# Attention inverses spread by transfer, a reordered hand-over to the MLP, a later record of sums and earlier sums for the last MLP group

## The chip, the cores and the metric

One core of a Trainium2 chip runs the whole program. The metric is the time of one execution on the device in microseconds; the median of three runs is 951.97 us (951.22 to 953.68). The engines are named as the profile names them: PE is TensorE (its matrix products; PEld its weight loads), DVE is VectorE, ACT is ScalarE, POOL is GpSimd, SP is SyncE, which here only issues transfers. A letter q behind an engine's name means its instruction queue.

## The reference

A batch of B = 16 sequences of S = 256 tokens with D = 256 features passes three attention layers and one MLP. All have H = 16 heads of 16 features; all numbers are 32-bit.

```python
# layer 0: cross attention to y, with RMS norms
x = rmsnorm(x + softmax(rms(x) Wq (rms(y) Wk)^T / 4) (rms(y) Wv) Wo)
# layer 1: causal self attention, layer norm, biases, rotary positions
x = x + attn(ln1(x), ln1(x), causal) @ sa_wo + sa_bo
# layer 2: cross attention to y, layer norm, biases, rotary positions
x = x + attn(ln2(x), y) @ ca_wo + ca_bo
# MLP: 256 -> 1024 -> 256
x = x + gelu(ln3(x) @ fc1_w + fc1_b) @ fc2_w + fc2_b
```

The layers follow one another for each sequence, but the sequences are independent.

## The kernel before, in words

There are 48 attentions, three for each sequence. `ORDER` fixes by hand in which order their layers come, so that attention i+1, i+2 and so on always belong to other sequences and can be prepared while attention i runs. No scheduler reorders anything: each engine executes its instructions in the order in which the loops issue them, and waits at each one until its operands are there.

**One attention** (`class Att`). Queries and keys are kept with features on the partitions: `qm` holds each query twice with every second head set to zero, `kT` the keys. `scores(n)` does one block: 8 products into two PSUM tiles `S` (two such pairs of banks exist, so a new block needs the exponentials of the block before last), ACT writes the exponentials to `pt`, and for the causal layer POOL zeroes what lies above the diagonal (L494). `values(n)` multiplies `pt` with `va`, the values of a head with a column of ones behind them, into the single PSUM bank `A`, so that the row 16 of each head's 32 rows is the sum of the exponentials. ACT copies `A` to `av` (L529). A cross attention has 4 such blocks, a causal one 3.

**Division by the sums.** The sums lie in 8 of the 128 rows of `av`. They are sent to memory (`hop[0]`, L530) and read back as a dense tile `sums` of 128 x 32 (L539); eight more transfers (L544) collect the unnormalized outputs into `oT`, features on partitions. `invert` takes the reciprocals on DVE (L554), adds `sums` to the record `seen` on POOL (L555), writes the reciprocals to `hop[1]` (L556) and reads them into one row out of 16 of the tile `first` (L560). `divide` repeats each such row over the 16 rows of its head by a stream shuffle on DVE (L566) and multiplies `oT` (L570). `project` multiplies with the output weights (L307) and adds to `x` (L576, L579). `seen` is examined once, in the MLP: if a sum was not finite, a second, safe version of the attentions runs instead.

**The loop over attentions.** Step i runs the blocks of attention i and between them, on all engines, pieces of its neighbours: after block 0 the finishing of i-3, statistics and normalization of i+2, `divide` of i-2 and the queries of i+1; after block 1 the keys of i+1; after the last but one the values of i+1 and `invert` of i-1; after the last `project` of i-2 and the transposes (`turn`) of i+2. Queries and keys go through a chain on DVE after their product (L406 to L435: shuffle, two multiplications with the rotary tables, an addition, for queries two more), and the next step's first scores need both. The last values of an attention run in the step after it.

**The MLP** works on groups of two sequences (`class Mlp`, 8 groups), both products split by Strassen's scheme with seven products instead of eight: `up(1)` to `up(7)` and `down(1)` to `down(7)`. Each has a normalization (`stats`, `norm`), transposes into `hT` (`turn`), and a `mix` of four subtractions on DVE (L672). The `up` products share PSUM banks: `X` and `Z` are summed into by several products and read between them; ACT copies a partial result out (`keep_sum`, L695), DVE adds to one (`add_sum`, L700), ACT applies GELU (L707). `sum_a(1)` to `sum_a(4)` are the DVE sums of GELU results (L757) that the `down` products need. `down` also sums into a bank `X` (the bank `A`) and a bank `Z`, which DVE reads after each product (`begin`, L779; `end`, L783). The products `up` of the next group run ahead of the `down` products of this one; the last group has none to run ahead. The end of the attentions and the first MLP groups are joined by hand: `mlps[0].stats()` and `norm()` in step 46, its `turn` and `mix` in step 47, `mlps[1].stats()` and `norm()` at its end, then the `up` products of group 0 with `project` of attention 46 between them, `turn` of group 1, its `up` products with `project` of attention 47 between them.

## Time and profile before

| | |
|---|---|
| runs, median (lowest to highest) | 951.97 us (951.22 to 953.68) |
| profiled execution | 953.16 us, of it 951.4 us span |
| PE busy | 936.1 us, 98% of the span |
| DVE, ACT, POOL busy | 666.0, 571.9, 294.6 us |
| shuffle of the inverses, DVE L566 | 48 x 0.742 us |
| record of sums, POOL L555 | 48 x 0.320 us; 280.4 us idle just before them |
| share of time in which the 16 DMA engines are busy, 40 to 720 us | 0.18 |
| from the last attention's first scores to the first `down` product | 721.10 to 767.14 us |

The profile is one execution. Its span runs from the first to the last instruction. A busy PE is not PE at its peak: its products are pipelined and their ends are modelled, so the distance between the starts of neighbouring groups says more than the busy share. Idle time of an engine that does not hold the others up costs nothing.

### The profile page before, as it was taken

The numbers are of one execution on the slowest core, as the hardware profiler recorded it, in microseconds if no ns is written. First come the engines' busy times: TensorE is split into PE (matmuls) and PEld (weight loads), VectorE is DVE, ScalarE is ACT, GpSimd is POOL, SyncE is SP. The second block draws the span as 40 slices with busy tenths as digits, with TensorE's granted clock in tenths as the row PEclk, the third lists the DMA queues.
The fourth block names the chain that finished last, engine by engine and source line by source line (L and its number), as shares of the span: only waits on it lengthen the run. The fifth ranks groups of instructions, "written<-read, shape, count | busy, mean of one in ns | idle before, by whom it ended". The sixth has DMA issues, their size and how long they took to land.

```text
span 951.4 us, 30022 instructions
## 1 busy us (share of the span) xinstructions
PE 936.1 (98%) x12374; PEld 551.6 (58%) x12374; DVE 666.0 (70%) x1483; ACT 571.9 (60%) x821; POOL 294.6 (31%) x502
## 2 busy tenths in 40 slices
PE   8999999999999999999999999999999899999997
PEld 4444455445454545455454445445445699999997
DVE  4347768877776797677866768787776776667653
ACT  4666666766666766666766676666676634444440
POOL 4213454334334344144242423334112211222200
PEclk9999999999999999999999999999999999999999
DMA  9531221202121122110222101010101000000001
GB/s 316 171 97 29 78 71 32 71 18 79 25 70 28 42 54 73 24 33 19 72 71 74 32 22 27 19 29 21 26 21 26 13 24 23 13 12 23 23 24 47
DMA packets 66089, 46.96 MB, mean 49 GB/s; under 512 B 25364, under 2 KB 65044, under 8 KB 65944
## 3 DMA queue, kind: packets, MB, share of 16 engines
q1 hardware_dynamic: 64712, 43.89, 16.8%
q8 instruction: 100, 1.64, 0.7%
q10 hardware_dynamic: 1232, 1.07, 0.4%
q14 instruction: 45, 0.37, 0.1%
HBM read 26.54 MB, written 5.79 MB: 34 GB/s over the span
## 4 chain that ended last, share of the span: by engine, by line
PE 88%; DVE 5%; DMA 3%; POOL 1%; ACT 1%; issue 1%; SPq 0%; DVEq 0%; POOLq 0%
PE S L476 18%; PE A L515 17%; PE d L294 16%; PE d L307 15%; PE A L762 6%; PE upX L676 6%; PE downZ L762 3%; PE upZ L676 3%; PE d L274 2%; PE d L762 2%; PE d L676 1%; DMA hop<-av 1%; DVE a L410 1%; PE d L657 1%; DVE u L410 1%
## 5 line engine op out<-in xcount | busy, mean ns | idle before, releaser
L487 ACT ACTIVATE pt<-S 128x1024 f32<-128x1024 f32 x224 | 217.4, 1022 | 114.3 <-PE S L476 114.3
L476 PE MATMUL S<-qm,kT 32*128 32x512 f32 (+1 forms) x1536 | 202.9, 600 | 2.1 <-DVE kT L435 1.0
L515 PE MATMUL A<-pt,va 128*32 128x256 f32 (+1 forms) x3072 | 193.0, 367 | 1.3 <-POOL pt L494 0.8
L515 PEld LDWEIGHTS A<-pt,va 128*32 128x32 f32 x3072 | 80.5, 109 | 158.5 <-issue 95.4
L487 ACT ACTIVATE pt<-S,sy 128x1024 f32<-128x1024 f32 x128 | 135.7, 1111 | 46.1 <-PE S L476 44.0
L555 POOL TENSOR_TENSOR seen<-seen,sums 128x64 f32<-128x64 f32 x48 | 15.4, 320 | 280.4 <-DVE sums L554 185.8
L476 PEld LDWEIGHTS S<-qm,kT 32*128 32x128 f32 x1536 | 62.4, 183 | 68.5 <-issue 25.4
L494 POOL TENSOR_SCALAR_AFFINE_SELECT pt<-pt 128x512 f32<-128x512 f32 x128 | 88.5, 713 | 27.4 <-ACT pt L487 27.3
L283 POOL TENSOR_TENSOR cur<-cur,bias 128x512 f32<-128x512 f32 x48 | 65.3, 1365 | 58.9 <-DVE xn L263 58.9
L402 ACT ACTIVATE a<-d,qk_bias 128x256 f32<-128x256 f32 x128 | 53.8, 471 | 38.5 <-PE d L294 33.4
L294 PE MATMUL d<-hT,sa 128*32 128x256 f32 x1024 | 63.1, 379 | 0.0
L238 POOL TENSOR_SCALAR r_ln<-bmv 128x2 f32<-128x2 f32 x48 | 12.6, 261 | 153.3 <-DVE bmv L257 152.6
L529 ACT COPY av<-A 128x512 f32<-128x512 f32 x96 | 56.6, 590 | 3.5 <-PE A L515 3.2
L410 DVE TENSOR_TENSOR u<-u,turn 128x512 f32<-128x512 f32 x64 | 53.5, 836 | 0.0
L410 DVE TENSOR_TENSOR a<-a,turn 128x512 f32<-128x512 f32 x64 | 50.2, 784 | 2.2
L263 DVE TENSOR_SCALAR xn<-cur,bmv,r_ln 128x256 f32<-128x256 f32 x96 | 51.1, 579 | 0.8 <-POOL r_ln L239 0.6
L707 ACT ACTIVATE g<-g,fb 128x256 f32<-128x256 f32 x96 | 40.9, 497 | 15.4 <-DVE g L700 15.4
L579 DVE TENSOR_TENSOR cur<-d,cur 128x512 f32<-128x512 f32 x32 | 21.7, 679 | 38.8 <-PE d L307 38.7
L406 DVE STREAM_SHUFFLE u<-a 128x512 f32<-128x512 f32 x64 | 47.7, 746 | 0.0
L294 PEld LDWEIGHTS d<-hT,sa 128*32 128x32 f32 x1024 | 34.3, 110 | 22.1
L695 ACT COPY g<-upX 128x512 f32<-128x512 f32 x32 | 17.2, 589 | 46.8 <-issue 39.0
L757 DVE TENSOR_TENSOR g<-g,g 128x512 f32<-128x512 f32 x64 | 40.7, 681 | 0.0
(142 smaller groups left out, 1568.1 us busy)
## 6 DMA issues: line engine op xcount, KB each, us to landing
oT<-av SPq DMA_DIRECT2D x384, 32.0 KB
cur<-in_x SPq DMA_DIRECT2D x16, 256.0 KB
xT<-in_xt SPq DMA_DIRECT2D x16, 256.0 KB
yT<-in_yt SPq DMA_DIRECT2D x16, 256.0 KB
y<-in_y SPq DMA_DIRECT2D x16, 256.0 KB
out<-res SPq DMA_DIRECT2D x15, 256.0 KB
fc<-in_fc SPq DMA_DIRECT2D x2, 1024.0 KB
rq<-rq_hop SPq DMA_DIRECT2D x14, 128.0 KB
```

Of the source, the lines that this page charges most:

```text
L283: nc.gpsimd.tensor_tensor(t, t, bias_sb[:, row : row + D].unsqueeze(1).to_broadcast([P, NC, D]), ALU.add)
L294: nc.tensor.matmul(ps[j : j + 32, t * S : (t + 1) * S], lhsT=w[:, k, at + t * P + j : at + t * P + j + 32], rhs=src[:, k, :], start=(k == ...
L307: nc.tensor.matmul(ps[j : j + 32, c * D : (c + 1) * D], lhsT=src[:, k, c * P + j : c * P + j + 32], rhs=w[:, k, at : at + D], start=(k == ...
L402: nc.scalar.activation(a[:, t], ps[:, t], AF.Identity, bias=bias[:, t : t + 1])
L410: nc.vector.tensor_tensor(t, t, table.unsqueeze(1).to_broadcast([P, KC, S]), ALU.mult)
L476: nc.tensor.matmul(ps[:, j, 2 * m * u : 2 * m * (u + 1)] .rearrange("p (i s) -> p i s", i=2), lhsT=self.kT[r, t, kc * P : (kc + 1) * P], r ...
L487: nc.scalar.activation(pt[:, :, :w], ps[:, :, :w], AF.Exp, scale=scale)
L494: nc.gpsimd.affine_select(out=diag, in_=diag, compare_op=ALU.is_ge, fill=0.0, base=0, pattern=[[0, 2], [0, 2], [1, P]], channel_multiplier=-1,
L515: nc.tensor.matmul(self.av[32 * r : 32 * r + 32, i, q0:S], lhsT=self.va[:, kc, 8 * t + 2 * r + i, :], rhs=pts[r // 2][:, r % 2, i * m : (i ...
L529: nc.scalar.copy(av, self.av)
L676: nc.tensor.matmul(banks[c // 2][:, (c % 2) * S : (c % 2 + 1) * S], lhsT=a[:, c * P : (c + 1) * P], rhs=b, start=(first and c % 2 == 0), s ...
L762: nc.tensor.matmul(ps[:, c, :], lhsT=a[f // 2][:, f % 2, c * P : (c + 1) * P], rhs=b[:, f, :], start=(first and c == 0 and f == 0), stop=True,
```

## The change

Four things are changed.

- **Inverses.** The tile `first` and the shuffle are gone. `invert` now reads `hop[1]` back with two transfers, one for each 128 features, which repeat each head's row of 256 inverses over 16 partitions: two times 128 x 256 numbers in place of 16 rows of 256. `divide` multiplies `oT` with this tile.
- **Record of sums.** The addition to `seen` moves from `invert` to `divide`, about one step later.
- **The end of the attentions.** The statistics, normalization and transposes of MLP groups 0 and 1 come one or two places earlier (steps 45, 46 and 47), their transposes are copied out of PSUM by DVE instead of ACT, `up(2)` of group 0 runs inside the last attention, `project` of attention 45 moves from the last block of step 47 to its second, and the `up` products, GELUs, `mix` and divisions behind the loop are put in a new order. `up(1)` and `up(2)` can now come in either order (`keep_or_add`). GELUs are named as steps of their own (`ups`).
- **The last group.** Its `sum_a(1)` to `sum_a(3)` are issued between the `down` products of the group before, in tiles of other tags.

The warm-up products at the start read a tile of zeros that is allocated later, as `first` is gone.

```diff
-    firsts = []
-    for i in range(2):
-        first = ctile([P, KC, S], f"first_{i}")
-        nc.gpsimd.memset(first, 0.0)
-        firsts.append(first)
     dram = ctx.enter_context(tc.tile_pool(name="dram", bufs=2, space=bass.MemoryType.DRAM))
     vas = [ctile([P, NC, H, 32], f"va_{i}") for i in range(2)]
...
+    zeros = work.tile([P, 512], F32, tag="inv", name="zeros")
+    nc.gpsimd.memset(zeros, 0.0)
     idle = dense_ps()
     for n in range(2):
         nc.tensor.matmul(
-            idle, lhsT=ident, rhs=firsts[0].rearrange("p t s -> p (t s)"), start=True, stop=True
+            idle, lhsT=ident, rhs=zeros, start=True, stop=True
         )
...
             if self.layer == 0:
                 nc.vector.tensor_scalar(sums[:, 0], sums[:, 0], 1e-30, None, ALU.max)
             nc.vector.reciprocal(sums[:, 1], sums[:, 0])
-            nc.gpsimd.tensor_tensor(seen, seen, sums, ALU.add)
             nc.sync.dma_start(
                 out=self.hop[1].rearrange("t g (a b) -> (t g a) b", b=2 * H), in_=sums[:, 1]
             )
-            self.first = firsts[self.i % 2]
-            nc.sync.dma_start(
-                out=self.first[0:P:HD], in_=self.hop[1].rearrange("t g q -> g t q")
-            )
+            self.inv = work.tile([P, KC, S], F32, tag="inv", name="inv")
+            for t in range(KC):
+                nc.sync.dma_start(
+                    out=self.inv[:, t],
+                    in_=self.hop[1, t].unsqueeze(1).to_broadcast([8, HD, S]),
+                )
         def divide(self):
-            inv = work.tile([P, KC, S], F32, tag="inv", name="inv", bufs=1)
-            nc.vector.stream_shuffle(
-                inv.rearrange("p t s -> p (t s)"),
-                self.first.rearrange("p t s -> p (t s)"), FIRST,
-            )
-            nc.vector.tensor_tensor(self.oT, self.oT, inv, ALU.mult)
+            nc.gpsimd.tensor_tensor(seen, seen, self.sums, ALU.add)
+            nc.vector.tensor_tensor(self.oT, self.oT, self.inv, ALU.mult)
         def project(self):
             res = by_token(self.oT, self.w_o, 0)
...
+            self.a = {}
             self.xs = [rows_of(2 * g + i) for i in range(2)]
         def stats(self):
...
-        def turn(self):
+        def turn(self, copy=nc.scalar.copy):
             self.hT = self.pool.tile([P, KC, 2, S], F32, tag="qm", name="hT3")
             for i, xn in enumerate(self.xns):
                 ps = dense_ps()
...
-                nc.scalar.copy(self.hT[:, :, i, :], ps.rearrange("p (k s) -> p k s", s=S))
-        def mix(self):
+                copy(self.hT[:, :, i, :], ps.rearrange("p (k s) -> p k s", s=S))
+        def mix(self, tag="av"):
             b = self.hT
-            self.ts = self.pool.tile([P, 4, S], F32, tag="av", name="ts")
-            t1, t2, t3, t4 = (self.ts[:, i] for i in range(4))
+            if tag == "av":
+                ts = self.pool.tile([P, 4, S], F32, tag=tag, name="ts")
+                self.ts = [ts[:, i] for i in range(4)]
+            else:
+                pairs = [self.pool.tile([P, 2, S], F32, tag=tag, name="ts") for _ in range(2)]
+                self.ts = [t[:, i] for t in pairs for i in range(2)]
+            t1, t2, t3, t4 = self.ts
             for o, x, y in (
                 (t1, b[:, 0, 1], b[:, 0, 0]), (t2, b[:, 1, 1], t1),
                 (t3, b[:, 1, 1], b[:, 0, 1]), (t4, b[:, 1, 0], t2),
...
-        def half(self, i, j):
+        def half(self, i, j, tag=None):
+            if tag is not None:
+                t = self.pool.tile([P, 4, S], F32, tag=tag, name=f"g{i}{j}")
+                return [t[:, 0:2], t[:, 2:4]]
             if i == 0:
                 return [
                     self.pool.tile([P, 2, S], F32, tag="yT", name=f"g{i}{j}", bufs=Y_LIVE)
...
-        def gelu(self, i, j, banks=None):
+        def keep_or_add(self, i, j, banks):
+            (self.add_sum if (i, j) in self.a else self.keep_sum)(i, j, banks)
+        def gelu(self, i, j):
+            banks = self.X if (i, j) == (0, 1) else None
             for c in range(4):
                 t = self.a[i, j][c // 2][:, c % 2]
                 src = t if banks is None else banks[c // 2][:, (c % 2) * S : (c % 2 + 1) * S]
...
         def up(self, n):
-            b, ts = self.hT, self.ts
+            b, ts = self.hT, getattr(self, "ts", None)
             if n == 1:
-                self.a = {}
                 self.X = psS.tile([P, 2, 512], F32, tag="S", name="upX")
                 self.X = [self.X[:, i] for i in range(2)]
                 self.up_product(1, self.X, up_a(0, 0), b[:, 0, 0], True)
-                self.keep_sum(0, 0, self.X)
+                self.keep_or_add(0, 0, self.X)
             elif n == 5:
                 self.Z = psS.tile([P, 2, 512], F32, tag="S", name="upZ")
                 self.Z = [self.Z[:, i] for i in range(2)]
-                self.up_product(5, self.Z, up_s[0], ts[:, 0], True)
+                self.up_product(5, self.Z, up_s[0], ts[0], True)
                 self.keep_sum(1, 1, self.Z)
             elif n == 6:
-                self.up_product(6, self.X, up_s[1], ts[:, 1], False)
+                self.up_product(6, self.X, up_s[1], ts[1], False)
                 self.keep_sum(1, 0, self.X)
             elif n == 2:
                 w = [dense_ps() for _ in range(2)]
                 self.up_product(2, w, up_a(0, 1), b[:, 1, 0], True)
-                self.add_sum(0, 0, w)
-                self.gelu(0, 0)
+                self.keep_or_add(0, 0, w)
             elif n == 7:
-                self.up_product(7, self.X, up_a(1, 0), ts[:, 2], False)
+                self.up_product(7, self.X, up_a(1, 0), ts[2], False)
                 self.add_sum(1, 1, self.X)
-                self.gelu(1, 1)
             elif n == 3:
                 self.up_product(3, self.Z, up_s[2], b[:, 1, 1], False)
                 self.add_sum(1, 0, self.Z)
-                self.gelu(1, 0)
             elif n == 4:
-                self.up_product(4, self.X, up_a(1, 1), ts[:, 3], False)
+                self.up_product(4, self.X, up_a(1, 1), ts[3], False)
                 self.a[0, 1] = self.half(0, 1)
-                self.gelu(0, 1, self.X)
-        def sum_a(self, n):
+        def ups(self, *steps):
+            for n in steps:
+                if isinstance(n, tuple):
+                    self.gelu(*n)
+                else:
+                    self.up(n)
+        def sum_a(self, n, tags=(None, None)):
             if n == 1:
-                self.s = {1: self.half(1, 2), 2: self.half(1, 3), 3: self.a[1, 0]}
+                self.s = {1: self.half(1, 2, tags[0]), 2: self.half(1, 3, tags[1])}
+                self.s[3] = self.a[1, 0]
                 self.s[4] = self.s[2]
             x, y, op = {
                 1: (self.a[1, 0], self.a[1, 1], ALU.add),
...
                     do(i - 2, "divide")
                     if not finishing:
                         do(i + 2, "norm")
+                    if i == N_ATT - 3:
+                        mlps[0].stats()
+                    if i == N_ATT - 2:
+                        mlps[0].norm()
+                    if i == N_ATT - 1:
+                        mlps[0].turn(nc.vector.tensor_copy)
                     do(i + 1, "q")
                 elif n == 1:
                     do(i + 1, "k")
...
                         do(i + 2, "norm")
                     for j in kept.get(i, ()):
                         att(j).keep()
+                    if i == N_ATT - 1:
+                        do(i - 2, "project")
+                        mlps[1].norm()
                 if n == final - 1:
                     do(i + 1, "v")
                     do(i - 1, "invert")
                     do(i + 2, "send")
+                    if i == N_ATT - 2:
+                        mlps[1].stats()
+                    if i == N_ATT - 1:
+                        mlps[0].up(2)
+                        mlps[0].mix("hT")
                 if n == final:
-                    do(i - 2, "project")
+                    if i == N_ATT - 1:
+                        mlps[1].turn(nc.vector.tensor_copy)
+                    else:
+                        do(i - 2, "project")
                     do(i + 2, "turn", "receive")
                 if i == 0 and n == 0:
                     load(4)
...
                     fold_gain(fc1_sb, slice(0, FF), V_G3, [i // 8])
                 if n == 1 and i > 8 and not a.causal:
                     next(combined, None)
-                if i == N_ATT - 2 and n == 1:
-                    mlps[0].stats()
-                    mlps[0].norm()
-                if i == N_ATT - 1 and n == 2:
-                    mlps[0].turn()
-                    mlps[0].mix()
-                if i == N_ATT - 1 and n == 3:
-                    mlps[1].stats()
-                    mlps[1].norm()
         last = att(N_ATT - 1)
         last.values(-1)
+        mlps[0].up(1)
         do(N_ATT - 2, "divide")
-        for n in (1, 5, 6, 2):
-            mlps[0].up(n)
+        mlps[0].ups(5, 6, (0, 0))
         do(N_ATT - 2, "project")
+        mlps[1].mix()
         last.invert()
-        for n in (7, 3, 4):
-            mlps[0].up(n)
-        mlps[1].turn()
-        mlps[1].mix()
+        mlps[0].ups(7, (1, 1), 3, 4, (0, 1), (1, 0))
         for g in range(B // 2):
             this = mlps[g]
             ahead, next_but_one = (mlps[i] if i < B // 2 else None for i in (g + 1, g + 2))
-            if ahead is not None:
+            if g == 0:
+                ahead.ups(2, 1)
+            elif ahead is not None:
                 ahead.up(1)
-            this.sum_a(1)
             if g == 0:
                 last.divide()
+            if ahead is not None:
+                this.sum_a(1)
             if next_but_one is not None:
                 next_but_one.stats()
             if ahead is not None:
-                ahead.up(5)
-                ahead.up(6)
-            this.sum_a(2)
+                ahead.ups(5, 6)
+                this.sum_a(2)
+            if g == 0:
+                ahead.gelu(0, 0)
+                last.project()
+            elif ahead is not None:
+                ahead.ups(2, (0, 0))
             if ahead is not None:
-                ahead.up(2)
-            if g == 0:
-                last.project()
-            if ahead is not None:
-                ahead.up(7)
-                ahead.up(3)
-                ahead.up(4)
-            this.sum_a(3)
+                ahead.ups(7, (1, 1), 3, (1, 0), 4, (0, 1))
+                this.sum_a(3)
             this.down(1)
+            final = g == B // 2 - 2
             if next_but_one is not None:
                 next_but_one.norm()
+            if final:
+                ahead.sum_a(1, ("qm", "av"))
             this.down(5)
+            if final:
+                ahead.sum_a(2)
             this.down(6)
             this.sum_a(4)
             this.down(2)
             if next_but_one is not None:
                 next_but_one.turn()
                 next_but_one.mix()
+            if final:
+                ahead.sum_a(3)
             this.down(7)
             this.down(3)
             this.down(4)
```

More of the change, by code (lines that the diff above doesn't have):

```diff
@@ L42 @@
 NROW = 6 * D
-FIRST = [i // HD * HD for i in range(32)]
 SWAP = [(i // HD) * HD + (i + HD // 2) % HD for i in range(32)]
@@ L1029, in xattn_kernel @@
                 m.mix()
-                for n in (1, 5, 6, 2, 7, 3, 4):
-                    m.up(n)
+                m.ups(1, 5, 6, 2, (0, 0), 7, (1, 1), 3, (1, 0), 4, (0, 1))
                 for n in (1, 2, 3):
```

## The prediction

> **What bounds the kernel now.** I read the page's first two parts, then the instructions in order of time at the places where TensorE's rows stand apart, then who waited for whom. The first two parts:
>
> ```profile
> span 951.4 us, 30022 instructions
> PE 936.1 (98%) x12374; PEld 551.6 (58%) x12374; DVE 666.0 (70%) x1483; ACT 571.9 (60%) x821; POOL 294.6 (31%) x502
> PEclk9999999999999999999999999999999999999999
> ```
>
> TensorE is busy almost throughout and its granted clock never drops; no other engine is above 70%. Since the changed kernel has the same products, each as long as before, only time in which TensorE does not advance can be won. To see it, I compare the distance between the starts of neighbouring groups with the same distance where nothing waits: a score group (S) 1.07 us, a value group (A) 0.89, a projection 1.84, an `up` product 1.73, eight transposes 0.87. Almost all groups keep these distances. The time lost sits in three places. First, from the last attention to the first `down` product:
>
> ```profile
> 721.10 1.14 PE L476 MATMUL S<-qm,kT 32*128 32x512 f32 x8
> 723.41 2.04 PE L476 MATMUL S<-qm,kT 32*128 32x512 f32 x8 [0.17 <-ACT pt L487]
> ...
> 739.68 1.89 PE L676 MATMUL d<-hT,fc 128*128 128x256 f32 x8
> 742.86 1.93 PE L307 MATMUL d<-cao,oT 128*32 128x256 f32 x32 [1.29 <-issue]
> 750.01 1.04 PE L657 MATMUL d<-ident,xn 128*128 128x128 f32 x8
> 752.88 1.99 PE L676 MATMUL upX<-hT,fc 128*128 128x256 f32 x8 [1.84 <-ACT hT L661]
> 767.14 1.95 PE L762 MATMUL A<-fc,g 128*128 128x128 f32 x16
> ```
>
> Columns: start, duration, engine, line, operation, count, and in brackets the idle time and its releaser. The second score group took 2.04 us where 1.14 is usual, because it waited for the exponentials; 739.68 to 742.86 is 3.19 us for a 1.73 us step; 750.01 to 752.88 is 2.87 for 0.87. Second, the value groups that follow a causal mask:
>
> ```profile
> 343.23 0.32 POOL L555 TENSOR_TENSOR seen<-seen,sums 128x64 f32<-128x64 f32 x1 [3.77 <-DVE sums L554]
> 343.50 1.41 POOL L494 TENSOR_SCALAR_AFFINE_SELECT pt<-pt 128x512 f32<-128x512 f32 x2
> 344.97 0.36 PEld L515 LDWEIGHTS A<-pt,va 128*32 128x32 f32 x10 [0.56 <-POOL pt L494]
> ```
>
> GpSimd stands 3.77 us at `seen`, waiting for VectorE's reciprocals; the two masks behind it come late, and the value group's weight load waits for them. Third, the boundary into the last MLP group:
>
> ```profile
> 933.30 3.69 DVE L757 TENSOR_TENSOR g<-g,g 128x512 f32<-128x512 f32 x6
> 933.53 2.02 PE L762 MATMUL A<-fc,g 128*128 128x128 f32 x16 [0.61 <-DVE res L779]
> 937.38 2.05 PE L762 MATMUL A<-down_t,g 128*128 128x128 f32 x16
> ```
>
> Last, the rows that the new transfer must be priced from:
>
> ```profile
> 300.62 0.64 SPq L560 DMA_DIRECT2D first<-hop  x1
> 302.65 0.01 DVE L566 LOAD_MASK_SELECT inv<-first  x1 [0.85 <-DMA first<-hop]
> 303.53 0.32 SPq L379 DMA_DIRECT2D rq<-rq_hop  x1
> 306.75 1.41 DVE L421 SCALAR_TENSOR_TENSOR qm<-d,vec,rq 128x512 f32<-128x512 f32 x2 [1.65 <-DMA rq<-rq_hop]
> 627.49 1.14 PE L476 MATMUL S<-qm,kT 32*128 32x512 f32 x8 [1.01 <-DVE kT L435]
> ```
>
> `first` (16 rows of 1 KB) is there 2.03 us after its issue; `rq` (one row repeated into 128 partitions, 128 KB) takes 3.22 us. VectorE waits for `first` 21 times. The last line is the one place where VectorE's chain already holds TensorE.
>
> **The change, part by part.**
>
> *The reordered end, from the last attention's first scores (721.10) to the first `down` product (767.14).* The same groups lie between these ends before and after: 4 S, 5 A, 2 sets of transposes, 3 projections, 14 `up` products: 4x1.07 + 5x0.89 + 2x0.87 + 3x1.84 + 14x1.73 = 40.2 us, against 46.04. So 5.8 us is stall. I walked the new order with the durations of the trace. The last attention's gaps are filled by transposes, a projection and an `up` product, so each score group comes 2.8 to 3.8 us after the last, and ScalarE needs 1.94 us for a pair of exponentials and 0.59 for a copy: no wait (1.9 us won). The projection of the last attention but one found `oT` undivided until 742.76, because VectorE did eight statistics and four normalizations first; now the second group's statistics run an attention and its normalizations two blocks earlier, and the division can be done at about 738.5, ahead of a projection at 740.5 (1.4 won). The 2.0 us at 750.01 came from copies queued on ScalarE behind twelve GELUs; they go to VectorE before that. Late next: the `up` product that reuses bank X waits for the VectorE additions (0.1 to 0.7), and the second MLP's first bank waits for the GELU that reads it (0 to 0.7). I take 0.8 left: **-5.0** (ends -5.8 and -2.0, the latter if both hand-overs stall again).
>
> *What moves into attentions 45 and 46.* The first group's statistics go to step 45 and its normalizations behind step 46's first block, the second group's statistics behind 46's key chain. Four pairs of statistics are 2.2 us of VectorE (717.24 to 719.45), four normalizations 2.3. Attention 46's keys are ready 4.35 us, 47's 3.78 us before the scores that read them, and VectorE idles 3.14 us ahead of 710.73. Two GpSimd additions (1.27 each) fall into idle time. **0**; without that slack it would be up to 0.8.
>
> *`seen` moved to the division.* There its sums are an attention old, so the 0.32 us runs without a wait. From the start of the value pair behind the last mask to the next product, ten causal attentions take 1.32 us and six take 2.49, 1.61, 1.93, 1.80, 1.41 and 1.75 (from 104.92, 343.83, 447.68, 522.37, 597.48, 628.56): 3.07 too much. I take **-2.8**; ends -3.1 and 0 (the exponentials would then be what came last).
>
> *The repeated inverse by transfer.* Removed: 48 shuffles of 0.745 us (35.6 us of VectorE), which as such win nothing beside TensorE. One issue on SyncE becomes two (0.32 us as `rq`, or 0.64 as `first`), ahead of the next `hop` and `oT` issues; SyncE usually idles after it (704.75 to 709.59), so 0, at worst a few tenths. The trace has no such transfer. From below: as quick as `first`, 2.0 us. The nearest row is `rq`, of the same size and also a repeated row: 3.0 to 3.2 us alone, 4.1 to 4.5 us with input loads beside it. The second of two issued 0.32 us apart, running beside the first, is there after 3.4 us; one after the other, 4.5 or more. The multiplication began 2.03+0.75 = 2.8 us after the issue where VectorE waited, and would begin 3.4 after: 0.6 us later, and where VectorE was late anyway, up to 0.75 earlier. I moved VectorE's rows by this, in order, letting each idle time absorb the delay, and counted what came after the scores' start (normally 0.15 us after the keys). Tight are the keys ending at 627.34 (slack 0.15), 446.42 (0.18), 89.55 (0.39), 595.7 and 342.1 (0.7). Arrival after 2.9 us costs 0.2, 3.4 costs 1.3, 4.0 costs 4.7, 4.5 costs 8.5, 5.0 costs 17 us, because a late division then also delays the next reciprocal. I take 3.4: **+1.4**; ends -0.7 (the stall at 627.49 shrinks) and +17.
>
> The Trainium skill, "DMA: Bandwidth & Descriptors", section "Anatomy of one DMA — SWDGE (gpsimd) path", gives a DMA about 2.0 us plus its bytes at 436 GB/s; `first` at 2.03 agrees, `rq` at 3.22 does not. By it two times 128 KB would be there after an estimated 2.6 to 2.9 us, and the sum would be -7.9 us. The same page's "Rules for kernel authors" speaks against the change: the slowest dimension of the access patterns sets how many engines share a transfer, and one below 16 confines it; this source has 8 there, so 8 engines would carry it, by which an estimated 1.5 us of extra transfer would bring 4.9 us and the sum to about +8.
>
> *The last group's sums.* The 0.77 us ahead of 933.53 stays: that product waits for VectorE to read bank A after the group before, which is not changed. 935.39 to 937.38 (1.99) and 937.38 to 939.26 (1.88) against 1.79 go: **-0.3**; ends 0 and -0.3.
>
> *The start.* The warm-up products read a tile zeroed later on GpSimd. They ended at 5.74 and the next product waited until 6.09, so up to 0.35 us of delay is covered: **0**, at worst 0.3.
>
> Sum: -5.0 - 2.8 + 1.4 - 0.3 = -6.7 us. The profiled execution took 953.16 us (951.4 of span, 1.8 around it): 946.5. It is 1.2 us above the median of the runs, so the median should be **945.3 us**.
>
> **The rivals.** *Slower: the repeated rows arrive too late.* For it: `rq` with loads beside it took 4.1 to 4.5 us, and here two are always in flight, each row read 16 times. Against: single `rq`s took 3.0 to 3.2, and DMA queues are busy only 18% between 40 and 720 us. Arrival after 4.45 us costs the 8.1 us that the rest wins; after 5.0 us the sum is +9, 961 us. Place: keys against scores at 89, 342, 446, 595, 627, 657 us. Chance 0.11.
>
> *No difference: arrival between 4.0 and 4.6 us.* Cost 4.7 to 9: sum -3.4 to +0.9, about 950.5. Chance 0.12.
>
> *The end does not close.* TensorE is stopped again at the hand-over, by VectorE's longer list (copies, additions, divisions, mixing) or by bank X: 2 instead of 5 us, 948.3, still faster. For it: 0.7 us are foreseen at each bank. Against: all reads walked above come out 0.2 to 2 us early. Chance 0.17.
>
> **How the numbers follow.** Forecast 0.60, with -5.8 - 3.1 - 0.7 - 0.3 = -9.9 us as its best end (942.1) and, with 4.0 us arrival, 948.6 as its worst. A measurement of this kernel tells about 0.3%, 2.9 us, from nothing; the forecast and the third rival are beyond it: faster 0.77, same 0.12, slower 0.11. The range is 942.5 to 951.9: it takes in both faster cases and most of the second rival, and leaves out the first.
>
> **What would show it.** Right: TensorE from the last attention's first scores to the first `down` product in 40.5 to 42 us; no GpSimd wait at `seen`, and the value pair behind each last mask 1.32 us; `oT` multiplied about 3.4 us after the first `inv` issue where VectorE waits; scores waiting for keys 1 to 2.5 us in all; 0.77 us still ahead of the last group. Wrong: `inv` arriving after 4.5 us with score groups waiting for keys at many attentions, or a new gap at the projections or at bank X after the last attention.

## The result and the profile after

The changed kernel takes 956.67 us (median of 7 runs, 954.49 to 958.23) against 951.54 for the kernel before (7 runs, 950.77 to 954.17). The medians differ by 5.1 us. The ratio of the runs, by which all comparisons go here, is 1.0046, with a 95% interval of 1.0031 to 1.0062: slower by 4.4 us (2.9 to 5.9), where 6.7 us less were forecast.

The first two parts of the page of the changed kernel:

```profile
span 954.2 us, 29935 instructions
PE 935.1 (98%) x12374; PEld 552.5 (58%) x12374; DVE 626.1 (66%) x1391; ACT 569.1 (60%) x817; POOL 293.0 (31%) x501
PEclk9999999999999999999999999999999999999999
```

VectorE is busy 40 us less, of which 35.6 are the shuffles, and TensorE is as busy as before: what grew is its waits and, in one place that is shown below, the time of its products. I cut both profiles at the same instructions (first scores of attentions 0, 4, 11 and 47, then the first `down` product; sections in us, the last one up to the end of the last product, the experiments beside them).

| | first scores at | 4 to 11 | 11 to 47 | 47 to first `down` | from there |
|---|---|---|---|---|---|
| before | 10.89 | 104.76 | 541.60 | 46.03 | 179.44 |
| changed | 11.59 | 106.45 | 544.30 | 43.96 | 179.13 |
| changed, shuffle again (e1) | 11.02 | 102.69 | 537.91 | 42.76 | 179.13 |
| before, transfer only (e2) | 11.18 | 111.00 | 546.04 | 45.64 | 179.44 |
| before, record moved only (e6) | 11.42 | 103.06 | 538.07 | 46.39 | 179.78 |
| before, hand-over and last group only (e9) | 11.62 | 103.93 | 541.94 | 42.76 | 179.13 |
| e1 with a small spare transfer (e10) | 10.73 | 107.01 | 537.88 | 42.76 | 179.14 |
| e1 with the shuffle done twice (e11) | 11.38 | 104.42 | 542.64 | 45.17 | 179.13 |

The last two sections became shorter, as foreseen; the attentions became longer. The start moved between 10.73 and 11.90 us in these and the other profiles, with old and new warm-up tiles alike, so it tells nothing of the change. The section 4 to 11, in which input loads still run, also differs by some us between profiles of like kernels, and little is rested on it.

Who waits, from the list of waits of the changed kernel (total, times, longest):

```profile
POOL seen L562 <- DVE sums L550: 18.7, 2, 12.9
PE S L472 <- DVE kT L431: 6.5, 7, 2.0
PE d L303 <- DVE oT L563: 1.5, 1, 1.5
```

Scores waited 1.0 us for VectorE's keys before, once; now 6.5 us in seven places, and a projection waits 1.5 us for `oT`. GpSimd's waits at `seen` (280 us before) are gone but for the last ones.

A step ahead of a layer 0 attention, in order of time; it answers to the rows of 300.62 to 306.75 of before:

```profile
303.42 1.30 SPq L556 DMA_DIRECT2D inv<-hop  x2
305.13 1.14 SPq L367 DMA_DIRECT2D rq_hop<-pad  x2
307.46 0.69 DVE L563 TENSOR_TENSOR oT<-oT,inv 128x512 f32<-128x512 f32 x1 [3.32 <-DMA rq_hop<-pad]
307.49 0.32 SPq L375 DMA_DIRECT2D rq<-rq_hop  x1
310.83 1.41 DVE L417 SCALAR_TENSOR_TENSOR qm<-d,vec,rq 128x512 f32<-128x512 f32 x2 [1.68 <-DMA rq<-rq_hop]
```

Two things are late. The multiplication begins 4.04 us after the issue (2.82 before, after the shuffle); over all steps in which VectorE stood idle just before it the median is 3.89 us, the least 3.42, and these are 45 of 48 steps instead of 21. In 37 of the 45 the multiplication begins within 0.4 us of the last completion of `inv`; in seven of the other eight VectorE came late itself and idles only 0.19 us.

The bracket names `rq_hop`, as the last transfer to land, but the semaphore records of this step show that `inv` decided: its last completion came at 307.14, and behind it stood three short instructions of VectorE's queue that only wait for semaphores (the multiplication waits for eight, of the transfers into `oT` and `inv`), some 0.1 us each. In the kernel before, these instructions ran beside the shuffle (302.66 to 302.97, the shuffle 302.65 to 303.40). So up to 0.4 us of the lateness is not the transfer's.

And `rq` is issued 4.07 us after the inverses instead of 2.91 (median over the steps 3.87): SyncE is held by the second issue, and the small transfers of `rq_hop`, which `rq` waits for, land later behind the repeated rows (`rq` is issued 1.21 to 1.49 us after their last issue ends; 1.04 to 1.22 before, but for one step).

The value group behind the last mask, at the attention where it came 0.29 us late before:

```profile
343.41 1.84 POOL L490 TENSOR_SCALAR_AFFINE_SELECT pt<-pt 128x512 f32<-128x512 f32 x2 [1.40 <-ACT pt L483]
344.79 1.00 DVE L431 TENSOR_TENSOR kT<-a,u 128x512 f32<-128x512 f32 x1
345.94 1.14 PE L472 MATMUL S<-qm,kT 32*128 32x512 f32 x8 [0.82 <-DVE kT L431]
347.01 1.02 PEld L511 LDWEIGHTS A<-pt,va 128*32 128x32 f32 x32 [0.76 <-issue]
```

The masks now run as soon as the exponentials are there (1.40 us of waiting for ScalarE, none at `seen`), and the weight load no longer waits for them: 15 of the 16 value pairs take 1.32 us. But the wait has come back one step earlier: the score group ahead of the pair waits 0.82 us for keys. The keys' last operation takes 1.00 us beside the mask where it takes 0.69 alone; this did not occur in the kernel before (0 of 32 key operations beside a mask; 4 of 32 here). It does not make the wait: with the shuffle again (e1 below) 4 of 32 are as long, and these score groups wait for nothing.

The sixteenth pair takes 2.56 us (from its start to the next product, as the others are measured), for another reason:

```profile
631.43 1.37 PE L472 MATMUL S<-qm,kT 32*128 32x512 f32 x8 [2.02 <-DVE kT L431]
632.73 2.79 PE L511 MATMUL A<-pt,va 128*32 128x128 f32 x32
637.29 1.14 PE L472 MATMUL S<-qm,kT 32*128 32x512 f32 x8
```

TensorE's granted clock was 0.5 from 632.21 on, for 3.41 us, behind the longest wait for keys. (The row of 9s above hides it, since its slices are 24 us long; between 630 and 640 us the mean granted clock is 0.83.) From this score group to the next takes 5.86 us, against 4.24 in e1 (623.17 to 627.41), so this stretch costs 1.6 us by itself. Of the profiled executions, this one and all others whose multiplication waits for a repeating transfer (e2, e4, e5, e7, e12, e13) have such stretches while products run, of 3.41 or 6.83 us; the kernel before, e1, e6, e8, e9, e10 and e11 have none. What exactly sets one off is not shown: it follows a wait of 2.02 us here and one of 1.74 in e2, but not one of 2.25 in e11 or of 1.84 in the kernel before (752.88).

The hand-over, TensorE alone:

```profile
726.14 1.14 PE L472 MATMUL S<-qm,kT 32*128 32x512 f32 x8 [0.53 <-DVE kT L431]
730.42 1.07 PE L511 MATMUL A<-pt,va 128*32 128x256 f32 x16
732.94 1.93 PE L303 MATMUL d<-cao,oT 128*32 128x256 f32 x32 [1.46 <-DVE oT L563]
741.90 1.19 PE L511 MATMUL A<-pt,va 128*32 128x256 f32 x16
770.10 1.95 PE L773 MATMUL A<-fc,g 128*128 128x128 f32 x16
```

The three stalls of before (second scores, last projection but one, copies behind GELUs) are gone. A new one of 1.46 us stands at the moved projection: the inverses were issued at 728.31 and multiplied at 732.19.

The boundary into the last group:

```profile
936.50 2.02 PE L773 MATMUL A<-fc,g 128*128 128x128 f32 x16 [0.61 <-DVE res L790]
938.35 1.95 PE L773 MATMUL downZ<-down_t,g 128*128 128x128 f32 x16
940.14 1.95 PE L773 MATMUL A<-down_t,g 128*128 128x128 f32 x16
```

The read of bank A still holds it; the two smaller waits behind it are gone.

### The profile page after: what moved, and what is told of

It reads as the page before. It is cut to its first block, busy times and chain, and to the rows that moved or that the text cites. A ratio compares the mean times of both kernels' runs of the same rounds, so it can differ in the third digit from the quotient of the medians.

```text
span 954.2 us, 29935 instructions
## 1 busy us (share of the span) xinstructions
PE 935.1 (98%) x12374; PEld 552.5 (58%) x12374; DVE 626.1 (66%) x1391; ACT 569.1 (60%) x817; POOL 293.0 (31%) x501
## 4 chain that ended last, share of the span: by engine, by line
PE 62%; DVE 19%; DMA 11%; SPq 3%; issue 2%; POOL 1%; ACT 1%; DVEq 0%; POOLq 0%
PE S L472 11%; PE A L511 10%; PE d L290 10%; PE d L303 9%; PE A L773 6%; PE upX L675 6%; DMA hop<-sums 3%; DMA inv<-hop 3%; DVE u L406 3%; PE downZ L773 3%; DVE a L406 3%; PE upZ L675 3%; DVE u L402 3%; DMA hop<-av 2%; DVE qm L424 2%
## 5 line engine op out<-in xcount | busy, mean ns | idle before, releaser
L511 PE MATMUL A<-pt,va 128*32 128x256 f32 (+1 forms) x3072 | 190.7, 369 | 0.0
L563 DVE TENSOR_TENSOR oT<-oT,inv 128x512 f32<-128x512 f32 x48 | 37.4, 779 | 105.2 <-DMA hop<-av 46.2
L417 DVE SCALAR_TENSOR_TENSOR qm<-d,vec,rq 128x512 f32<-128x512 f32 x32 | 22.5, 746 | 36.9 <-DMA rq<-rq_hop 31.8
L259 DVE TENSOR_SCALAR xn<-cur,bmv,r_ln 128x256 f32<-128x256 f32 x96 | 46.3, 531 | 0.0
L234 POOL TENSOR_SCALAR r_o<-ms_o 128x2 f32<-128x2 f32 x16 | 4.7, 292 | 129.1 <-DVE sq L242 119.0
```

What stands on the lines that cost most here:

```text
L511: nc.tensor.matmul(self.av[32 * r : 32 * r + 32, i, q0:S], lhsT=self.va[:, kc, 8 * t + 2 * r + i, :], rhs=pts[r // 2][:, r % 2, i * m : (i ...
```

## The experiments

Theory A: the repeated rows reach VectorE too late, and what follows the late multiplication (keys, projections) stops TensorE. Theory B: the other parts make the loss. Later, theory C: the loss comes from SyncE's queue, held by the longer issues, and D: from the traffic. Ratios are to the kernel before in the same comparison, with 95% intervals. That kernel ran again in each comparison (medians of 951.5 to 953.9 us), so differences between two experiments are taken from their ratios and not from their times.

**e1: the shuffle again, the rest of the change kept.**

```diff
-            self.inv = work.tile([P, KC, S], F32, tag="inv", name="inv")
-            for t in range(KC):
-                nc.sync.dma_start(out=self.inv[:, t], in_=self.hop[1, t]...to_broadcast([8, HD, S]))
+            nc.sync.dma_start(out=self.first[0:P:HD], in_=self.hop[1].rearrange("t g q -> g t q"))
...
+            nc.vector.stream_shuffle(inv..., self.first..., FIRST)
```

> The changed kernel with the inverses as before (one transfer into one row of 16, shuffle on VectorE, and with them the old zeros at the start); the moved record, the new hand-over and the last group's sums stay. Theory A, the repeated rows arrive too late (measured in the changed kernel's trace: the multiplication begins 3.4 to 4.2 us after the first issue where VectorE waits, against 2.7 to 2.9 with the shuffle; waits that follow on TensorE add up to about 8.8 us between 90 and 725 us, 1.5 at 731 us, 0.65 at the start): all of this comes back, profile about 945.5 us, run median 944 to 946, ratio 0.992 to 0.994; hand-over 42.3 to 42.6 us instead of 43.96; waits of scores for keys at most 1.5 us in all. Theory B, the loss is made by the other parts (record on GpSimd, VectorE's longer list at the end): 952 to 956.

Measured: 945.61 us, ratio 0.9929 (0.9915 to 0.9943). Hand-over 42.76 us, scores waiting for keys once:

```profile
PE S L476 <- DVE kT L435: 1.5, 1, 1.5
```

Theory B falls. The transfer of the inverses costs 1.0046 - 0.9929, 11 us, more than all that the other parts win. This version beats both kernels.

**e2: the kernel before with the transfer alone** (the same edit the other way round).

> The kernel before with only the inverses by transfer (and with it the later zeros at the start). Theory A: slower by 7 to 10 us, 959 to 962, with 0.65 us of it at the start and the stalls at projections and at scores behind keys. Theory B: within 2 us of before.

Measured: 962.97 us, ratio 1.0111 (1.0094 to 1.0128), 10.6 us slower; somewhat above what was expected. Here a second path shows, the list of waits of e2:

```profile
PEld A L511 <- POOL pt L490: 14.1, 21, 2.8
PE S L472 <- DVE kT L431: 3.5, 4, 1.7
```

With the record still behind the reciprocals, VectorE's lateness reaches TensorE mostly over GpSimd's masks (8.9 us and at most 0.9 at once in the kernel before), less over the keys. One stretch of 3.41 us at half the clock is in it too.

**e5: the second of the two transfers issued on ScalarE's queue.**

```diff
-                nc.sync.dma_start(
+                (nc.sync, nc.scalar)[t].dma_start(
```

> The changed kernel with the second of the two inverse transfers issued on ScalarE's queue instead of SyncE's. SyncE is then held 0.64 instead of 1.33 us. Theory A with the second transfer's late issue (0.69 us after the first) as the cause: where ScalarE is free the multiplication begins 2.9 to 3.3 us after the first issue and 3 to 5 us are won, 952 to 954; but ScalarE executes in order, and where the issue stands behind exponentials or holds them (0.64 us each, 48 times) time is lost: up to 10 us slower, 966. Theory C, what counts is that SyncE's queue is held and the issues behind it come late: 951 to 953 with the multiplication as late as before.

Measured: 1082.66 us, ratio 1.1371 (1.1336 to 1.1406). Far worse than the worst that was expected, for the reason named there, but I had priced only the issue and not the wait ahead of it. Waits of ScalarE in e5:

```profile
ACT pt L483 <- DMA hop<-sums: 105.0, 23, 8.2
```

The issue stands in order among the exponentials and waits for the reciprocals to reach memory; behind it the exponentials wait. In its profile 85 us ran at half the clock, by which an estimated 43 of its 131 us, at most, are TensorE's slower products. It decides nothing between A and C.

**e8: e1, with the two repeating transfers issued behind the early one, into a buffer that nobody reads.**

```diff
+            spare = dram.tile([KC, P, S], F32, tag="spare", name="spare")
+            for t in range(KC):
+                nc.sync.dma_start(out=spare[t], in_=self.hop[1, t].unsqueeze(1).to_broadcast([8, HD, S]))
```

> As the first of these runs (shuffle), but behind each transfer into one row of 16 the two repeating transfers are issued too, into a buffer in memory that nobody reads: SyncE's queue is held 1.96 us instead of 0.64, and the traffic is the same as in the changed kernel, but VectorE waits only for the early rows. Theory A (arrival): within 1.5 us of the first run. Theory C (queue held, or traffic): most of the 9 us comes back, 951 us or more.

Measured: 955.05 us, ratio 1.0025 (1.0014 to 1.0037): 9 us slower than e1, though the multiplication begins 2.87 us after the issue, as in e1 (2.83). Theory A alone falls: longer holding of SyncE, with traffic, is enough to lose as much. But this holds SyncE 1.3 us longer than e1, the changed kernel only 0.7.

**e10: e1, with one small spare transfer (16 KB).**

```diff
+            spare = dram.tile([8, KC, S], F32, tag="spare", name="spare")
+            nc.sync.dma_start(out=spare, in_=self.hop[1].rearrange("t g q -> g t q"))
```

> The kernel with the shuffle again (945.6 us), with a second small transfer of the same 16 KB behind each transfer into one row of 16, to a buffer in memory that nobody reads. SyncE's queue is held some 0.3 to 0.65 us longer 48 times, the traffic is 16 KB instead of 256 KB more, VectorE waits for nothing new. Theory C (queue): 948 to 951, with the projections and scores of the layers that need the root of the squares first late, since that transfer is issued behind. Theory A and theory D (arrival, traffic): within 1 us of 945.6.

Measured: 948.21 us, ratio 0.9948 (0.993 to 0.9967): 1.8 us above e1, with an interval that just holds zero. Its issue took 0.66 us, so SyncE was held as long as in the changed kernel. Rows of e10:

```profile
93.67 0.63 SPq L559 DMA_DIRECT2D first<-hop  x1
94.36 0.66 SPq L563 DMA_DIRECT2D spare<-hop  x1
97.26 0.32 SPq L379 DMA_DIRECT2D rq<-rq_hop  x1
122.07 1.14 PE L476 MATMUL S<-qm,kT 32*128 32x512 f32 x8 [2.03 <-DVE kT L435]
```

`rq` is issued 3.59 us after `first`, 2.92 in the same step of e1. In the table its whole loss lies between attentions 4 and 11 (107.01 against 102.69, in the section that varies), none between 11 and 47 (537.88 against 537.91). So a queue held this long costs, if anything, among the layer 0 attentions and nothing later: alone it can't be the cause of the changed kernel's 6.4 us between 11 and 47. (e8, with twice the extra holding and the traffic, loses 5.1 us there.)

**e11: e1, with the shuffle done twice.** SyncE and the traffic are untouched; the multiplication begins later.

```diff
-            nc.vector.stream_shuffle(inv..., self.first..., FIRST)
+            for n in range(2):
+                nc.vector.stream_shuffle(inv..., self.first..., FIRST)
```

> The kernel with the shuffle again (945.6 us), with the shuffle done twice: SyncE's issues and the traffic are unchanged, but the multiplication begins about 3.6 us after the issue instead of 2.83 where VectorE waits, and VectorE has 0.75 us more work at each attention. Theory A, the late multiplication costs by itself: 949 to 953, with new waits of scores for keys in the attentions that follow a layer 2 (22, 29, 39, 41, 42, 47) and at the projection in the last attention, and little in attentions 5 to 8. Theory C, only what stands behind on SyncE's queue costs: within 1.5 us of 945.6.

Measured: 954.15 us, ratio 1.0001 (0.9989 to 1.0014): 6.9 us slower than e1. The multiplication begins 3.67 us after the issue. List of waits of e11:

```profile
PE S L476 <- DVE kT L435: 6.7, 6, 2.3
PEld d L307 <- DVE oT L571: 2.8, 3, 1.7
```

These are the changed kernel's waits: between 11 and 47 it loses 4.7 us (542.64 against 537.91), with new or longer waits at attentions 22, 29, 39, 41 and 47 as expected (none at 42), and 2.4 in the hand-over, 1.44 of it at the same projection. The changed kernel's 6.4 us in that section less the 1.6 of its half clock are 4.8, the same. Theory A holds for this part. (VectorE also has 0.75 us more work at each attention, so this is the price of lateness and work together. And its runs fall into two groups, 951.2 to 953.6 us at a mean granted clock of 0.999 and 954.1 to 956.0 at 0.997 to 0.998; the profile is of the first.)

**e12: the changed kernel, multiplied in two halves, each behind its own transfer.**

```diff
-            nc.vector.tensor_tensor(self.oT, self.oT, self.inv, ALU.mult)
+            for t in range(KC):
+                nc.vector.tensor_tensor(self.oT[:, t], self.oT[:, t], self.inv[:, t], ALU.mult)
```

> The changed kernel with the multiplication by the inverses in two halves, each behind its own transfer: SyncE and the traffic are unchanged, the first half is multiplied while the second transfer is under way, and the product ends 0.2 to 0.35 us earlier. Theory A: 1 to 3 us faster than the changed kernel, 953.5 to 955.5. Theory C: no difference, 956 to 957.5.

Measured: 954.63 us, ratio 0.9997 (0.9977 to 1.0018): 4.7 us below the changed kernel (2 to 7 by the two intervals), outside what theory C allowed: earliness is worth something with SyncE and the traffic unchanged. How much is not shown. The twelve runs lie between 948.26 and 957.86, the mean granted clock with them (0.999 or 1.000 in the four fastest, 0.994 to 0.996 in the three slowest), and the profile is of one of the slow ones, 957.59, with 10.2 us at half the clock. In it the hand-over takes 42.31 us, without the stall of 1.46.

**e13: the changed kernel, with the small transfers of `rq_hop` issued ahead of the reciprocals.**

```diff
-                    do(i - 1, "invert")
                     do(i + 2, "send")
+                    do(i - 1, "invert")
```

> The changed kernel with the two small transfers of the inverse roots (rq_hop, only ahead of an attention of layer 0) issued ahead of the reciprocals' transfers instead of behind them. The repeated roots (rq) can then be issued some 1.3 us earlier, since they no longer wait for a transfer that was issued behind the repeated inverses; the inverses themselves are issued about 1.1 us later in these 14 steps. Theory C, the late rq makes the loss in attentions 5 to 10 (about 3.8 us): 2 to 4 us faster than the changed kernel, 952.5 to 954.5. Theory A, the arrival of the inverses makes it there too: 1 to 5 us slower, 958 to 962.

Measured: 956.53 us, ratio 1.0032 (1.0014 to 1.005), 1.3 us below the changed kernel with overlapping intervals: neither expectation. `rq` was issued 4.2 us after the reciprocals instead of 5.8 in the median, and nothing clear came of it. What the late `rq` costs in the changed kernel is therefore not separated from the late inverses there.

**e7: one repeating transfer of 128 rows of 2 KB in place of two of 1 KB** (the sums lie in memory with both halves of a head side by side).

```diff
-            for t in range(KC):
-                nc.sync.dma_start(out=self.inv[:, t], in_=self.hop[1, t].unsqueeze(1).to_broadcast([8, HD, S]))
+            nc.sync.dma_start(
+                out=self.inv.rearrange("p t s -> p (t s)"),
+                in_=self.hop[1].rearrange("g t q -> g (t q)").unsqueeze(1).to_broadcast([8, HD, KC * S]),
+            )
```

> The changed kernel with one repeating transfer in place of two: the sums lie in memory with both halves of a head's row side by side, so that one transfer brings 128 rows of 2 KB. Same bytes, one issue (about 0.64 us of SyncE in place of 1.33), rows there 0.1 to 0.3 us earlier than now. Theory A, the arrival sets the loss (it stays 3.2 to 3.6 us after the issue, against 2.8 with the shuffle): 952 to 955. Theory C, the time for which SyncE's queue is held sets it: 947 to 949. Theory D, the traffic sets it: 955 to 957, as the changed kernel.

Measured: 963.79 us, ratio 1.0114 (1.0094 to 1.0133), outside all three. The rows were there later, not earlier (multiplication 4.18 us after the issue in the median), and `rq` was issued 2.2 to 3.0 us after `rq_hop`'s last issue ended in all steps but one (1.21 to 1.49 in the changed kernel), since that landed behind the long rows. One issue fewer did not help; since lateness grew on both paths, it does not tell C from A.

**e4: the same with the reciprocals written twice, so that the transfer reads 16 source rows instead of 8.**

```diff
+            for h in range(2):
+                nc.sync.dma_start(out=self.twice[:, h].rearrange("g (a b) -> g a b", b=2 * H), in_=sums[:, 1])
+            nc.sync.dma_start(out=self.inv..., in_=self.twice.rearrange("g h q -> (g h) q")
+                .unsqueeze(1).to_broadcast([16, HD // 2, KC * S]))
```

> As the run with one repeating transfer, but the reciprocals are written to memory twice, side by side, so that the transfer reads 16 source rows, each eight times, in place of 8 rows sixteen times. One more small issue (about 0.37 us) on SyncE. If the number of source rows sets how many engines carry a transfer, it is 16 in place of 8, the transfer's own time falls from about 1.3 to 0.7 us, and the rows are there 2.5 to 2.8 us after the issue. Theory A (arrival): 946 to 948. Theory C (queue): 949 to 952. If the row count does not matter: arrival 3.2 us or more and slower than the run with one transfer.

Measured: 970.05 us, ratio 1.0178 (1.0157 to 1.0199): a miss. The two writes took 0.64 us each, not 0.37, and the read was issued 3.43 us after the reciprocals in the mean instead of 2.44. The transfer itself did what was asked: in the packet records, the 8-row source ends with 8 completion writes and the 16-row source with 16, and the multiplication begins 3.51 instead of 4.18 us after the issue.

**e6 and e9: the record alone, and the hand-over with the last group alone, on the kernel before.**

```diff
-            nc.gpsimd.tensor_tensor(seen, seen, sums, ALU.add)
...
         def divide(self):
+            nc.gpsimd.tensor_tensor(seen, seen, self.sums, ALU.add)
```

> The kernel before with only the record of sums moved to the division. From the trace: the six value pairs that took 1.41 to 2.49 us take 1.32, 3.07 us less. Theory (GpSimd's wait holds the masks): 948.5 to 950, ratio 0.997. Rival, a later wait takes it back (scores for keys, with VectorE unchanged): within 0.1% of before.

> The kernel before with only the new hand-over to the MLP and the last group's earlier sums (inverses by shuffle, record of sums behind the reciprocals). From the trace of the first run: the hand-over takes 42.8 instead of 46.0 us, the last group 0.3 us less: 948 to 949.5, ratio 0.996 to 0.997. Rival, the earlier statistics delay keys in attentions 46 and 47: 950 to 952.

Measured: e6 950.09 us, ratio 0.9976 (0.9964 to 0.9988), 2.3 us won; e9 950.26 us, ratio 0.9963 (0.9944 to 0.9983), 3.5 us won. e6's rival falls. e9's named 950 to 952 us, which holds 950.26, but the kernel before took 953.92 in that comparison; by the ratio, and by its hand-over of 42.76 us, which is e1's, it falls too. The parts add up: -2.3 - 3.5 + 10.6 (e2) = +4.8 against +4.4 measured.

## Why the prediction was wrong

**The repeated inverse: three terms mis-sized, and with them the sign.** +1.4 was foreseen, 11 measured.
- "The second of two issued 0.32 us apart ... is there after 3.4 us" failed in its price for the issue. I took `rq`'s 0.32 us; these issues take 0.64, as `first` did. In the records of the changed kernel the first rows come 1.41 us after the issue, the last completion of the first transfer reaches its semaphore at 2.75 us in the median and that of the second at 3.57 (at the earliest 3.38), and VectorE's waiting instructions add up to 0.4. 3.4 was the best case and not the usual one, 3.89.
- "SyncE usually idles after it ..., so 0, at worst a few tenths" failed. I named `hop` and `oT` as what is queued behind and overlooked `rq_hop` and `rq`, on which the layer 0 queries wait. e10 puts 1.8 us (-0.4 to 4) on the held queue alone, e8 9 us on twice the extra holding with the traffic.
- The price of lateness failed most. Between the 1.3 us at 3.4 and the 4.7 at 4.0 that it gave, 3.89 lies at about 4 us and 3.67 at about 3; e11 lost 6.9 at 3.67. The replay moved VectorE's rows alone and counted only scores that wait for keys. It left out the projections that wait for `oT` (1.46 us at 732.94) and the bank that a late query multiplication keeps (1.01 us at 102.64, a projection waiting for `qm`; 0.42 at 101.40 before, which the prediction passed over), and it kept each later row's length. That products stay "each as long as before" failed too, by the 1.6 us at half the clock. Whether VectorE's idle times, which I let absorb the delay, were themselves moved by it was not tried.

**The slower rival had the right mechanism at the wrong place.** It was put at 4.45 us and later; 3.89 was enough. The sentence on the Trainium skill, "DMA: Bandwidth & Descriptors", section "Rules for kernel authors", which came to about +8 us, was nearer than the forecast, but by luck: it put the arrival at 4.9 us, which by the prediction's own prices costs some 15 and makes +7, and the arrival was 3.89. Its rule on the slowest dimension agrees with the 8 and 16 completion writes. The 2.0 us plus bytes at 436 GB/s of the same page's "Anatomy of one DMA — SWDGE (gpsimd) path" does not fit: 2.6 to 2.9 us by it, 3.42 at the least here. That section speaks of transfers that GpSimd issues; these are issued by SyncE.

**`seen`: right.** -2.8 foreseen, -2.3 (-1.1 to -3.4) measured in e6, no wait left at `seen` but at the end, and the value pairs at 1.32 us. Not foreseen: the masks, no longer held up, now fall beside VectorE's key chain. The Trainium skill, "SBUF — State Buffer", section "Who interferes with whom", says that VectorE and GpSimd share one pair of ports as an exclusive lock, and that a VectorE instruction with two inputs in SBUF contends for it with a GpSimd instruction that reads SBUF. That they hinder each other agrees: the 0.69 us key operation with two operands from SBUF took 1.00 us and the rotary product 1.12 instead of 0.68 beside a mask. Whether it is a lock that one of them keeps these rows do not settle: the key operation took 1.00 us in all four cases, whether 0.46 or 0.82 us of it lay beside a mask.

**The hand-over: the mechanism right, the size too large.** All three stalls went, as walked, and in e1 the longest wait left is one of 0.18 us at a bank. Still it takes 42.76 us without a stall, not 41. The 40.2 us were made of undisturbed distances within one kind of work. Between kinds that alternate, each step took 0.1 to 0.2 us more: a value group 1.00 instead of 0.89, transposes 1.02 instead of 0.87, an `up` product often 1.83 instead of 1.73. In the changed kernel 1.2 us more go to the late inverses (43.96 against 42.76): the walk had used the division's time with the shuffle.

**The last group: right to a few hundredths.** 179.44 became 179.13 us, and the 0.77 us ahead of it stayed. **The start: 0**, as taken; it varies by itself by more than the price that was feared.

**Open.** How the 11 us divide between late inverses, the held queue and the traffic between attentions 4 and 11 is not settled; later it is the lateness, by e10 and e11, with the 1.6 us at half the clock that came with it. That the semaphore instructions ahead of the multiplication cost what their 0.4 us suggest was not tried.

## What to carry to other kernels

What counts of the work on an engine that is not the bound is when its result is there, not how long the engine is busy: 48 shuffles of 0.74 us left VectorE, the transfer that replaced them put the result 1.06 us later, and the kernel lost 11 us. Price a transfer by what stands behind it on its queue too, and by all the waits that a later operand causes, projections and banks as well as the next product; a replay of one engine's rows gave too low a price here. Look at the granted clock in short windows, since a row of 24 us slices can hide a stretch at half of it. Test the parts of a combined change one by one: three of the four together won 6.7 us here, and without the fourth the kernel is 0.7% faster than before.

## What the runs showed of the hardware

- A transfer whose access pattern has 8 as its outermost count ended with 8 completion writes (`inv` in e7, and `first`, whose 16 rows are 8 times 2) and one with 16 with 16 (e4); for the same 256 KB the last completion reached its semaphore 3.86 us after the issue in the first case and 3.32 in the second, in the median.
- In most steps 1.4 us pass from the issue to the first row, whatever the size (`first`, 16 KB; `inv`, 128 KB; 256 KB in one). From the last completion at the semaphore to the start of the multiplication 0.02 to 0.39 us pass in the changed kernel, by the number of semaphore instructions that still stand ahead of it.
- TensorE's granted clock was 0.5 for 3.41 us behind a wait of 2.02 us in the changed kernel, and the products of that stretch took 1.6 us longer.
- A transfer issued on a busy engine's queue stops that engine until its source is ready: 105 us of ScalarE in 23 waits in e5, which ran 14% longer (part of it at half the clock).
- VectorE's operations on two SBUF operands took 0.68 to 0.69 us with GpSimd idle, mostly 1.00 to 1.12 beside a GpSimd mask (some stayed at 0.69), and up to 1.78 beside other GpSimd instructions.
